# Four-layer network on one core: small VectorE steps of the two Mamba layers issued between a slot's product and its scan

## The chip, the cores and the metric

The kernel runs on one core of a Trainium2 chip (trn2). A core has five engines that run side by side, each in the order in which its own instructions were written, and each held up only by semaphores: TensorE (PE in the profile), VectorE (DVE), ScalarE (ACT), GpSimd (POOL) and SyncE (SP), which issues the transfers here. The metric is the device time of one execution in microseconds; lower is better. Three timed executions before the change took 11755.33, 11777.04 and 11796.26 us, the median is 11777.04 us.

## The reference, cut to what matters

Four images of 256 channels and 64x64 points go through four layers. Layers 0 and 1 are recurrences with windowed attention, which the change does not touch. Layer 2 is a Mamba layer with 512 inner channels, layer 3 runs one Mamba of 128 inner channels over four groups of 64 channels, with a small MLP and a convolution behind it. The core of both is this scan over the 4096 points, for 16 states n of every channel:

```
delta = softplus(dt @ dt_proj_w + dt_proj_b)
step:  h = exp(delta*A) * h + (delta*u) * B        # per state
       y = sum over states of h * C
y = (y + u*D) * silu(z)                            # the gate
```

In front of layer 2 and layer 3 stands a normalization over the channels, which subtracts the mean ("centring") and divides by the deviation.

## The kernel before, in words

An image goes through the layers alone; the four images follow one another. In both Mamba layers the points are cut into 4 chunks of 1024 (NC), and the inner channels of a chunk into 4 blocks of 128 partitions, so that a layer has 16 blocks. A block has 16 **slots**, one for each state: layer 2 and layer 3 of an image are 256 slots each, written out one after the other in `scan_blocks` (L907). A slot i is this work on [128, 1024] tiles:

- spread: TensorE copies row B of the state to all partitions, into a PSUM tile `pb` (L949); there are two such tiles, so spread(i+2) waits for scan(i).
- product: VectorE multiplies `pb` by `du` (delta times u) in place (L1019).
- decay: ScalarE computes `da` = exp(delta*A) three slots ahead (L961).
- scan: VectorE runs the recurrence over the 1024 points (L1025), reading `da` and `pb`.
- GpSimd multiplies the result `h` by C into `hc` (L1031); there are three `h` and three `hc` tiles.
- turn: TensorE adds `hc` into the PSUM tile `y` by eight transposes (L977), one slot later.

Three states of a block (0, 5, 10 in layer 2 and 0, 4, 8 in layer 3) are **apart**: their B row comes by a transfer, GpSimd does the product (L935), and the decay goes to PSUM as `dap`. Such a slot has no product on VectorE.

All other work is cut into small steps that are hung on slots by hand. `put(d, places, steps)` files a step under a slot number of a block; the loop runs the steps of a slot (`blk["bg"]`) after it has issued the slot's scan, so on VectorE such a step stands between the scan of its slot and the product of the next. A place n + 0.5 comes a little later in the slot. The steps that the change touches:

- `delta_steps` (L1139) makes delta for a later block in two halves of 512 columns: proj (a matmul into a PSUM tile `dt_ps`, then Abs, Exp and Ln on ScalarE, L1150 to L1152), add (one VectorE instruction, L1156, that reads `dt_ps`), and at last `times_u` (GpSimd, `du`, L1160).
- `end` (in `scan_blocks`) finishes the block before: at slot ends[0] ScalarE copies `y`; at slots ends[1] and ends[2] TensorE transposes a half back and adds u*D into a PSUM tile `fin_ps` (L998, L1002); one slot after each, VectorE multiplies it into the gate `zs` (L991). ends is (1, 2, 4) in layer 2 and (1, 2, 2) in layer 3.
- `norm_steps`: mean (matmul), center (VectorE, L1087, and a Square on ScalarE, L1093), deviation, scale, affine.
- `in_u` makes u of the next pair of blocks or chunk by matmuls (L1314 in layer 2, L1700 in layer 3), which a Silu, the x projection and delta of that block follow.

`dt_ps`, `fin_ps`, `u_ps`, `ln_pm`, `z_ps` and others share the PSUM tag "mm", which has two buffers. A matmul that needs one waits, and with it all that TensorE has behind it, until the last reader of the buffer's old content is done. In layer 3 `in_u` takes both at once:

```python
            def two(name):
                return [psum.tile([P, NT], F32, tag="mm", name=name) for g in range(2)]
```

Of the kernel before, what the change touches and what calls it, by code (L numbers as in the profile page):

```python
# [12 lines left out]
ALU = mybir.AluOpType  # L13
# [13 lines left out]
DS = 16  # L27
# [17 lines left out]
class Net:  # L45
# [858 lines left out]

    def scan_blocks(self, blocks, loop, psum, psb, psy, apart, ends, first, last={}):  # L907
        nc = self.nc
        slots = [(blk, n) for blk in blocks for n in range(DS)]
        halves = [slice(s, s + NT) for s in range(0, NC, NT)]  # L910
# [71 lines left out]

        def end(blk, n):
            if n == ends[0]:
                for ss in halves:
                    nc.scalar.activation(blk["du"][:, ss], blk["y"][:, ss], AF.Copy)
            for j, (ss, first) in enumerate(zip(halves, ends[1:])):
                if n == first + 1:  # L990
                    nc.vector.tensor_tensor(  # L991
                        blk["zs"][:, ss], blk["out", j], blk["zs"][:, ss], ALU.mult
                    )
                if n == first:
                    blk["out", j] = ps = psum.tile([P, NT], F32, tag="mm", name="fin_ps")
                    for i in range(NT // P):
                        t = slice(ss.start + i * P, ss.start + i * P + P)
                        nc.tensor.matmul(  # L998
                            ps[:, i * P : (i + 1) * P], blk["du"][:, t], self.ident,
                            is_transpose=True, start=(i == 0), stop=False,  # L1000
                        )
                    nc.tensor.matmul(ps, blk["diag_d"], blk["u"][:, ss], start=False, stop=True)  # L1002
# [14 lines left out]
        for i, (blk, n) in enumerate(slots):  # L1017
            if not is_apart(i):
                nc.vector.tensor_tensor(pb[i], blk["du"], pb[i], ALU.mult)  # L1019
            h[i] = loop.tile([P, NC], F32, tag="h", name="h", bufs=3)  # L1020
            for ss in pieces(i):
                state = 0.0 if blk["first"] else blk["state"](n)
                if ss.start:
                    state = h[i][:, ss.start - 1 : ss.start]
                nc.vector.tensor_tensor_scan(  # L1025
                    h[i][:, ss], da[i][:, ss], pb[i][:, ss], state, ALU.mult, ALU.add
                )
            product(i + 2)
            hc[i] = loop.tile([P, NC], F32, tag="hc", name="hc", bufs=3)
            for ss in pieces(i):  # L1030
                nc.gpsimd.tensor_tensor(hc[i][:, ss], h[i][:, ss], cb[i][:, ss], ALU.mult)  # L1031
            decay(i + 3)
            keep(i - 1)
            load_c(i + 3)
            load_b(i + 4)
            if i >= DS and n != ends[0]:
                end(slots[i - DS][0], n)
            for step in blk["bg"].get(n, ()):
                step()
            if i >= DS and n == ends[0]:  # L1040
                end(slots[i - DS][0], n)
            spread(i + 2)
            for step in blk["bg"].get(n + 0.5, ()):
                step()
            turn(i - 1)
            decay(i + 2, True)
            for d in (pb, da, cb):
                del d[i]
        turn(n_slot - 1)
        for n in range(ends[2] + 2):  # L1050
            end(blocks[-1], n)
            for f in last.get(n, ()):
                f()
# [168 lines left out]
    def mamba_layer(self, x, bridge, pe_dram, w_in, w_cw, w_x, w_dt, w_out, v_dram):  # L1222
        tc, nc = self.tc, self.nc
        ND = 4
        with ExitStack() as ctx:
# [232 lines left out]
            for k in range(n_chunk):  # L1458
# [3 lines left out]
                def put(d, where, steps):  # L1462
                    for i, f in zip(where, steps):
                        bg[d].setdefault(i, []).append(f)

                if k == 0:
                    put(0, (2, 3, 4, 5), folds)
                if k:
                    for i, where in enumerate(((3, 4, 5), (6, 7, 8), (9, 10, 11), (12, 13, 14))):
                        put(0, where, out_proj(k - 1, i // 2, i % 2))  # L1470
                put(0, (9, 10, 11, 12, 12), delta(k, 1))
                put(0, (14, 15), (in_z(k, 0, 0), in_z(k, 0, 1)))
                put(1, (1.5,), (silu((k, 0, "zs")),))
                put(1, (6, 7, 8, 9, 10), delta(k, 2))
                put(1, (11, 12), (in_z(k, 1, 0), in_z(k, 1, 1)))
                put(1, (14,), (silu((k, 1, "zs")),))
                at = (6, 7, 8, 9, 10) if more else (5, 6, 7, 8, 9)
                put(2, at, delta(k, 3))
                at = (10, 11) if more else (8, 9)
                put(2, at, (in_z(k, 2, 0), in_z(k, 2, 1)))  # L1480
                z3 = in_z(k, 3, 0), in_z(k, 3, 1)
# [4 lines left out]
                if more:  # L1486

                    if k == 0:
                        put(0, (0,), (lambda: begin(1),))
                        put(0, (0, 0, 1, 3, 4, 5, 6, 7), self.later(lambda: norm(1, 0), 8))  # L1490
                    h1 = self.later(lambda k=k: norm(k + 1, 1), 8)
                    if k:
                        put(0, (2, 4, 5, 7, 8, 13, 14, 15), h1)
                    else:
                        put(0, (7, 8, 9, 12, 13, 14, 15), h1[:7])
                        put(1, (1,), h1[7:])
                    if k + 2 < n_chunk:
                        put(3, (3,), (lambda k=k: begin(k + 2),))
                        h0 = self.later(lambda k=k: norm(k + 2, 0), 8)
                        put(3, (4, 6, 7, 14, 15), h0[:5])  # L1500
                        chunks[k + 1]["late"] = ((0, 1, 2), h0[5:])
                    if k:
                        put(0, *chunks[k]["late"])
                    u = all_u(k + 1)
                    put(1, range(5, 16), u[:11])
                    put(2, range(14), u[11:25])
                    put(3, (1, 2, 3, 4, 5, 5, 6), u[25:])
                    xs = x_proj(k + 1)
                    put(2, (13,), (silu((k + 1, 0, "u"), (k + 1, 1, "u"), (k + 1, 2, "u"),
                                        (k, 2, "zs")),))  # L1510
                    put(3, (7,), (silu((k + 1, 3, "u"), (k, 3, "zs")),))
                    put(3, (7, 8, 8, 9), xs)
                    put(3, (10, 11, 11, 12, 12), delta(k + 1, 0))
                    put(3, (10, 11, 12, 13), xs[4:])
                else:
                    put(2, (13,), (silu((k, 2, "zs"), (k, 3, "zs")),))

                    sums, about, square, squares, early_squares = stats

                    def square_into(i):  # L1520
                        tag, bufs = ("pe", 1) if i % 2 else ("u", 5)
                        square(i, work.tile([P, NC], F32, tag=tag, name="cs_sq", bufs=bufs))

                    for i in range(6):
                        put(1 + (13 + i) // DS, ((13 + i) % DS,), (lambda i=i: sums(i),))
                        put(2 + (12 + i) // DS, ((12 + i) % DS,), (lambda i=i: square_into(i),))
                        put(2 + (13 + i) // DS, ((13 + i) % DS,), (lambda i=i: squares(i),))
                    put(2, (3,), (about,))
                    put(3, (3,), (early_squares,))
                    for i in range(4):  # L1530
                        at = (6 + 2 * i, 7 + 2 * i)
                        put(3, at, out_proj(k, i // 2, i % 2, ((0, 1, 2),)))
# [18 lines left out]
            def center(s):  # L1551
# [6 lines left out]

            self.scan_blocks(
                [blk for c in chunks for blk in c["blocks"]], loop, psum, psb, psy, (0, 5, 10),  # L1560
                (1, 2, 4), (xs0[4:6], (), xs0[6:]),
                {1: [lambda: mean3(0)], 2: [lambda: center(0)], 4: [lambda: mean3(1)],
                 5: [lambda: center(1)]},
            )
            late_square, late_sums, late_squares, finish = late_stats
            sq3 = work.tile([P, 2, NC + 3], F32, tag="xn", name="ln_sq")
# [50 lines left out]
    def grouped_mamba_layer(self, x, bridge, begun, ws_dram, outc_dram, v_dram, out_b, load):  # L1617
        tc, nc = self.tc, self.nc
        w_in, w_cw, w_x, w_dt, w_out, w_f1, w_f2 = ws_dram
        with ExitStack() as ctx:  # L1620
# [359 lines left out]
            for i, (k, c) in enumerate(pairs):  # L1980
                even, odd = chunks[k]["blocks"][2 * c : 2 * c + 2]

                def put(blk, where, steps):
                    for i, f in zip(where, steps):
                        blk["bg"].setdefault(i, []).append(f)


                for where, steps in late:
                    put(even, where, steps)
# [3 lines left out]
                if more:  # L1993
                    h0, h1 = (self.later(lambda k=k, s=s: norm(k + 1, s), 5) for s in range(2))
                    put(even, (0,), (lambda k=k: begin(k + 1),))
                    put(even, (0, 1, 4, 5, 6), h0)
                    put(even, (14, 15), h1)
                    put(odd, (1, 2, 3), h1[2:])
                put(even, (4, 5, 9, 11, 12, 13) if i else (6, 7, 9, 11, 12, 13), x_proj(k, 2 * c + 1))
                if i:  # L2000
# [8 lines left out]
                        late.append(((0, 0.5, 1, 1), m1[4:]))  # L2009
                    else:  # L2010
                        put(odd, (3, 4, 4.5, 5, 6), m1[3:])
                put(even, (7, 9, 8, 9, 10) if i else (9, 10, 10, 11, 11), delta(k, 2 * c + 1))
                also = [lambda k=k: out_silu(k - 1)] if c == 1 and k else []
                if i == 0:
                    put(even, (1, 2), [in_z(0, 0, s) for s in range(2)])
# [13 lines left out]
                if i + 1 < len(pairs):  # L2029
# [1 line left out]
                    put(odd, (4, 5, 6, 7), all_u(nk, ncol))  # L2031
                    put(odd, (7,), (silu(nk, ncol, "u"),))
                    put(odd, (8, 8, 8, 9, 10, 11), x_proj(nk, 2 * ncol))
                    put(odd, (9, 11, 10, 11, 12), delta(nk, 2 * ncol))
                    put(odd, (13, 14), [in_z(nk, ncol, s) for s in range(2)])
            self.scan_blocks(
                [blk for c in chunks for blk in c["blocks"]], loop, psum, psb, psy, (0, 4, 8),
                (1, 2, 2), (xs0[2:4], (), xs0[4:]),
            )

            k, pair = n_chunk - 1, chunks[-1]["blocks"][2:]
# [160 lines left out]
```

## Time and profile before

| what | value |
|---|---|
| timed executions, median of 3 | 11777.04 us |
| the profiled execution, its own time | 11788.99 us |
| its span, first to last instruction | 11787.2 us |
| mean granted TensorE clock | 0.936 |
| busy TensorE, VectorE | 10026.0 us (85%), 9803.2 us (83%) |
| busy GpSimd, ScalarE | 8773.9 us (74%), 7025.7 us (60%) |
| scans of layer 2, first image | 978 to 1922 us of the span |
| scans of layer 3, first image | 1973 to 2923 us of the span |

The times are from one execution under the profiler, whose instructions are listed with start, length, the idle time of the engine before it, and what ended that idle time. An engine that is busy for a large share of the span need not set the time: what counts is which wait ends last in a stage. The two Mamba layers take 944 and 950 us of each image, so some 64% of the span over four images; the rest is attention.

### The profile page before, as it was taken

The numbers are of one execution on the slowest core, as the hardware profiler recorded it, in microseconds if no ns is written. First come the engines' busy times: TensorE is split into PE (matmuls) and PEld (weight loads), VectorE is DVE, ScalarE is ACT, GpSimd is POOL, SyncE is SP. The second block draws the span as 40 slices with busy tenths as digits, with TensorE's granted clock in tenths as the row PEclk, the third lists the DMA queues.
The fourth block names the chain that finished last, engine by engine and source line by source line (L and its number), as shares of the span: only waits on it lengthen the run. The fifth ranks groups of instructions, "written<-read, shape, count | busy, mean of one in ns | idle before, by whom it ended". The sixth has DMA issues, their size and how long they took to land. (4 is left out here: it accounts for less than half of the span.)

```text
span 11787.2 us, 192389 instructions
## 1 busy us (share of the span) xinstructions
PE 10026.0 (85%) x71104; PEld 5739.6 (49%) x71104; DVE 9803.2 (83%) x8342; ACT 7025.7 (60%) x13152; POOL 8773.9 (74%) x6070
## 2 busy tenths in 40 slices
PE   8998887777899888777789988877778998887787
PEld 4564554444456455444445645544444564554443
DVE  6677998998667799899866779989986677998998
ACT  4565555776456555577645655557764565555776
POOL 4666887898466688789846668878984666887897
PEclk9999998999999899899999989989999998998999
DMA  3344554454334455455433445545543354554554
GB/s 97 106 137 139 174 174 148 168 181 161 90 105 136 136 172 177 148 171 180 163 88 108 140 136 176 172 148 170 179 161 91 104 142 139 172 174 149 169 175 154
DMA packets 682507, 1742.11 MB, mean 148 GB/s; under 512 B 88896, under 2 KB 194896, under 8 KB 681312
## 3 DMA queue, kind: packets, MB, share of 16 engines
q1 hardware_dynamic: 676448, 1721.41, 44.9%
q8 instruction: 563, 9.22, 0.3%
q10 hardware_dynamic: 5120, 8.39, 0.3%
q14 instruction: 376, 3.08, 0.1%
HBM read 1601.52 MB, written 94.39 MB: 144 GB/s over the span
## 5 line engine op out<-in xcount | busy, mean ns | idle before, releaser
L1031 POOL TENSOR_TENSOR hc<-h,cb 128x1024 f32<-128x1024 f32 x2056 | 4809.8, 2351 | 785.8 <-DVE h L1025 332.9
L1025 DVE TENSOR_TENSOR_SCAN h<-da,m_state,pb 128x1024 f32<-128x1024 f32 x1248 | 2920.4, 2340 | 163.6 <-DVE pb L1019 3.4
L977 PE MATMUL y<-ident,hc 128*128 128x128 f32 x16384 | 2358.0, 292 | 413.2 <-POOL hc L1031 342.3
L977 PEld LDWEIGHTS y<-ident,hc 128*128 128x128 f32 x16384 | 2050.6, 151 | 1144.6 <-POOL hc L1031 598.5
L1019 DVE TENSOR_TENSOR pb<-du,pb 128x1024 f32<-128x1024 f32 x1672 | 2025.2, 1211 | 104.1 <-PE pb L949 97.4
L961 ACT ACTIVATE da<-delta,m_v 128x1024 f32<-128x1024 f32 x1672 | 1899.2, 1141 | 132.4 <-DVE h L1025 109.0
L949 PE MATMUL pb<-m_parts,pick 128*128 128x512 bf16 x3312 | 1083.0, 411 | 804.0 <-DVE h L1025 753.7
L603 POOL TENSOR_SCALAR pr<-pr,sm,zero 128x256 f32<-128x256 f32 x2048 | 1107.3, 556 | 384.5 <-DVE sm L600 380.3
L588 ACT ACTIVATE pr<-sc,mn 128x256 f32<-128x256 f32 x2048 | 953.1, 477 | 515.9 <-DVE sm L600 397.6
L949 PEld LDWEIGHTS <-pick 128*128 128x128 bf16 x3312 | 263.5, 101 | 1742.9 <-DVE h L1025 971.6
L577 DVE TENSOR_REDUCE mn<-sc 128x4 f32<-128x1024 f32 x512 | 630.1, 1232 | 536.1 <-PE sc L565 536.0
L1025 DVE TENSOR_TENSOR_SCAN h<-da,pb 128x1024 f32<-128x1024 f32 x424 | 969.7, 2287 | 54.5 <-DVE pb L1019 0.5
L935 POOL TENSOR_TENSOR bb<-du,bb 128x1024 f32<-128x1024 f32 x376 | 888.8, 2364 | 111.4 <-DMA bb<-m_cd 102.4
L1025 DVE TENSOR_TENSOR_SCAN h<-dap,m_state,bb 128x1024 f32<-128x1024 f32 x288 | 672.3, 2335 | 68.2 <-ACT dap L961 48.3
L252 PE MATMUL conv_ps<-att_y,att_wb 128*128 128x512 f32 x1536 | 685.9, 596 | 0.0
L616 PE MATMUL pt_ps<-ident,pr 128*128 128x128 f32 x4096 | 638.6, 292 | 41.9 <-POOL pr L603 21.8
L961 ACT ACTIVATE dap<-delta,m_v 128x1024 f32<-128x1024 f32 x376 | 419.8, 1117 | 313.7 <-DVE h L1025 232.2
L565 PE MATMUL sc<-kv,q_swap 32*64 32x128 f32 x8192 | 592.5, 282 | 15.6 <-DMA kv<-kv_dram 5.4
L565 PE MATMUL sc<-kv,att_y 32*64 32x128 f32 x7168 | 574.5, 282 | 33.3 <-DMA kv<-kv_dram 24.3
L616 PEld LDWEIGHTS pt_ps<-ident,pr 128*128 128x128 f32 x4096 | 459.5, 146 | 169.8 <-POOL pr L603 111.6
L290 DVE SCALAR_TENSOR_TENSOR lp<-vimg,att_v,lp 128x512 f32<-128x512 f32 x672 | 507.7, 756 | 30.8 <-DVE lp L290 1.0
L565 PEld LDWEIGHTS sc<-kv,att_y 32*64 32x64 f32 x7168 | 425.9, 136 | 165.2 <-ACT pr L588 76.6
(303 smaller groups left out, 17832.5 us busy)
## 6 DMA issues: line engine op xcount, KB each, us to landing
cb<-m_cd SPq DMA_DIRECT2D x2048, 512.0 KB, 3.9
kv<-kv_dram SPq DMA_DIRECT2D x1984, 128.0 KB, 2.8
bb<-m_cd SPq DMA_DIRECT2D x376, 512.0 KB, 5.1
kv_dram<-kst SPq DMA_DIRECT2D x128, 256.0 KB, 3.4
kv_dram<-vn SPq DMA_DIRECT2D x128, 256.0 KB, 4.1
q_swap<-att_y SPq DMA_DIRECT2D x96, 256.0 KB, 4.3
m_pe<-in_pe_dram SPq DMA_DIRECT2D x32, 512.0 KB, 5.9
out_dram<-yo SPq DMA_DIRECT2D x64, 256.0 KB, 2.4
```

What stands on the lines that cost most here:

```text
L252: nc.tensor.matmul(ps, w[:, k, w0 + m * P : w0 + (m + 1) * P], src[:, k], start=(k == 0), stop=(k == 1),)
L565: nc.tensor.matmul(sc[h][b * 64 : b * 64 + 64, r, w, m, :], (own(sj, m) if r == b else swap[sj % 2][:, m])[rows, 2 * a + w], kv[i, w][rows ...
L588: nc.scalar.activation(t[:, g].rearrange("p j r t -> p r j t"), sc[h][:, :, g // 2, g % 2, :].rearrange("p r (j t) -> p r j t", j=2), AF.E ...
L603: nc.gpsimd.tensor_scalar(t[:, g], t[:, g], s[:, g : g + 1], self.zero, ALU.mult, ALU.add)
L616: nc.tensor.transpose(pt[h][j][:, g, :], t[:, g, j].rearrange("p r t -> p (r t)"), self.ident,)
L935: nc.gpsimd.tensor_tensor(pb[i], slots[i][0]["du"], pb[i], ALU.mult)
L949: nc.tensor.matmul(pb[i][:, ss], self.pick[:, n : n + 1].to_broadcast([P, P]), blk["parts"][:, ss], start=True, stop=True,)
L961: nc.scalar.activation(da[i], blk["delta"], AF.Exp, scale=blk["a"](n))
L977: nc.tensor.matmul(blk["y"][:, ss], t[:, ss], self.ident, is_transpose=True, start=(n == 0 and ss.start % NT == 0), stop=(n == DS - 1 and ...
L1019: nc.vector.tensor_tensor(pb[i], blk["du"], pb[i], ALU.mult)
L1025: nc.vector.tensor_tensor_scan(h[i][:, ss], da[i][:, ss], pb[i][:, ss], state, ALU.mult, ALU.add)
L1031: nc.gpsimd.tensor_tensor(hc[i][:, ss], h[i][:, ss], cb[i][:, ss], ALU.mult)
```

## The change

In `scan_blocks` a new list of steps, filed under `("between", n)`, is run after slot n's product has been issued and before its scan; the gate products get a function of their own, run in the same place, with slots of their own (`gates`).

```diff
+        def gate(blk, n):
+            for j, (ss, at) in enumerate(zip(halves, gates)):
+                if n == at:
+                    nc.vector.tensor_tensor(
+                        blk["zs"][:, ss], blk["out", j], blk["zs"][:, ss], ALU.mult
+                    )
+
         def end(blk, n):
...
-                if n == first + 1:
-                    nc.vector.tensor_tensor(
-                        blk["zs"][:, ss], blk["out", j], blk["zs"][:, ss], ALU.mult
-                    )
...
             if not is_apart(i):
                 nc.vector.tensor_tensor(pb[i], blk["du"], pb[i], ALU.mult)
+            for step in blk["bg"].get(("between", n), ()):
+                step()
+            if i >= DS:
+                gate(slots[i - DS][0], n)
...
-        for n in range(ends[2] + 2):
+        for n in range(max(gates) + 1):
+            gate(blocks[-1], n)
             end(blocks[-1], n)
```

The two additions of delta, the gate products and some centrings are filed there. `soft` puts the five steps proj, add, proj, add, times_u, the two adds between:

```diff
+                def soft(d, places, steps):
+                    p0, a0, p1, a1, du = places
+                    put(d, (p0, ("between", a0), p1, ("between", a1), du), steps)
# layer 2
-                put(0, (9, 10, 11, 12, 12), delta(k, 1))
+                soft(0, (9, 11, 11, 13, 13), delta(k, 1))
-                put(1, (6, 7, 8, 9, 10), delta(k, 2))
+                soft(1, (6, 8, 8, 11, 11), delta(k, 2))
-                at = (6, 7, 8, 9, 10) if more else (5, 6, 7, 8, 9)
-                put(2, at, delta(k, 3))
+                at = (6, 8, 8, 10, 10) if more else (5, 7, 7, 9, 9)
+                soft(2, at, delta(k, 3))
-                        put(0, (2, 4, 5, 7, 8, 13, 14, 15), h1)
+                        put(0, (2, 4, 5, 7, ("between", 9), 13, 14, 15), h1)
-                        put(0, (7, 8, 9, 12, 13, 14, 15), h1[:7])
+                        put(0, (7, 8, 9, 12, ("between", 14), 14, 15), h1[:7])
-                    put(3, (10, 11, 11, 12, 12), delta(k + 1, 0))
+                    soft(3, (10, 12, 11, 13, 13), delta(k + 1, 0))
-                (1, 2, 4), (xs0[4:6], (), xs0[6:]),
+                (1, 2, 4), (4, 6), (xs0[4:6], (), xs0[6:]),
-                 5: [lambda: center(1)]},
+                 6: [lambda: center(1)]},
# layer 3
-                    put(even, (0, 1, 4, 5, 6), h0)
+                    put(even, (0, ("between", 2), 4, 5, 6), h0)
-                put(even, (7, 9, 8, 9, 10) if i else (9, 10, 10, 11, 11), delta(k, 2 * c + 1))
+                soft(even, (7, 9, 8, 10, 10) if i else (9, 11, 10, 12, 12), delta(k, 2 * c + 1))
-                    put(odd, (9, 11, 10, 11, 12), delta(nk, 2 * ncol))
+                    soft(odd, (9, 11, 10, 12, 12), delta(nk, 2 * ncol))
-                (1, 2, 2), (xs0[2:4], (), xs0[4:]),
+                (1, 2, 3), (4, 5), (xs0[2:4], (), xs0[4:]),
```

No instruction is added or removed and no tile changes its size; what changes is the order on VectorE, the slots of `times_u` in layer 2, and in layer 3 the slot of the second `fin_ps` and of its gate.

## The prediction

> **What bounds the kernel now.** I began with the page: busy shares, then the groups. The change works in the two Mamba layers alone, so what counts is what holds VectorE (DVE) between their scans.
>
> ```profile
> PE 10026.0 (85%) x71104; PEld 5739.6 (49%) x71104; DVE 9803.2 (83%) x8342; ACT 7025.7 (60%) x13152; POOL 8773.9 (74%) x6070
> L1025 DVE TENSOR_TENSOR_SCAN h<-da,m_state,pb 128x1024 f32<-128x1024 f32 x1248 | 2920.4, 2340 | 163.6 <-DVE pb L1019 3.4
> L1019 DVE TENSOR_TENSOR pb<-du,pb 128x1024 f32<-128x1024 f32 x1672 | 2025.2, 1211 | 104.1 <-PE pb L949 97.4
> ```
>
> The second line shows 163.6 us of idle time before 1248 scans, 131 ns each, of which only 3.4 us has a releaser: a gap in front of every scan that follows its product. The third shows that products wait for TensorE's spread, but only 97.4 us in all.
>
> The groups of VectorE with shapes kept apart show the steps that move. They stand idle for other engines before them:
>
> ```profile
> L1156 DVE SCALAR_TENSOR_TENSOR delta<-dt_ps,delta 128x512 f32<-128x512 f32 x256 | 171.6, 675 | 102.8 <-ACT delta L1152 102.8
> L991 DVE TENSOR_TENSOR m_zs<-fin_ps,m_zs 128x512 f32<-128x512 f32 x256 | 169.4, 674 | 56.1 <-PE fin_ps L1002 55.9
> ```
>
> The timeline of VectorE (start, length, both in us) shows the gap at close range:
>
> ```profile
> 1062.24 0.67 DVE L991 TENSOR_TENSOR m_zs<-fin_ps,m_zs 128x512 f32<-128x512 f32 x1
> 1062.83 1.22 DVE L1019 TENSOR_TENSOR pb<-du,pb 128x1024 f32<-128x1024 f32 x1
> 1064.18 2.29 DVE L1025 TENSOR_TENSOR_SCAN h<-da,pb 128x1024 f32<-128x1024 f32 x1
> 1066.38 2.26 DVE L1025 TENSOR_TENSOR_SCAN h<-dap,bb 128x1024 f32<-128x1024 f32 x1
> ```
>
> The gate ends at 1062.91, and the product starts 0.08 before that. The product ends at 1064.05, and the scan that reads it starts 0.13 later. The next scan starts 0.09 before the last one's end. So a pair of neighbours costs 0.21 to 0.22 us more when the second reads the first; I use 0.217 (133 ns after the end against 84 ns before it, the usual values along the timeline).
>
> Last, busy time by stretch, for one chunk (four blocks) of layer 2, cut where another engine takes over. Columns: stretch, its us, then busy us of PE, PEld, DVE, ACT, POOL, the clock, DMA.
>
> ```profile
> 4254.60:4351.80 97.20, 93.22 (x397) 52.35 (x398) 92.08 (x56) 52.85 (x83) 80.14 (x35) 0.98 0.51 173
> 4351.80:4379.20 27.40, 26.62 (x111) 15.54 (x112) 23.31 (x15) 13.18 (x24) 18.92 (x9) 0.94 0.50 181
> 4379.20:4425.70 46.50, 35.04 (x153) 20.72 (x152) 41.85 (x26) 28.88 (x45) 45.64 (x21) 0.89 0.51 167
> 4425.70:4490.60 64.90, 57.12 (x262) 33.32 (x260) 62.60 (x39) 39.34 (x62) 60.33 (x27) 0.97 0.51 179
> ```
>
> TensorE is full in the first two (in_u, 93.22 of 97.20 and 26.62 of 27.40), GpSimd in the third (45.64 of 46.50). VectorE sets the pace in the fourth alone: 65 of 236 us. That is the point of this case: VectorE's savings count only where nobody else is full.
>
> **The change, part by part.** *The swap.* Moved steps that get a product in front of them: in layer 2, per image, 27 adds, 30 gates and 3 centrings; in layer 3, 30 adds, 15 gates (the other 15 come before slot 4, which is apart and has no product) and 3 centrings. That is 108, over four images 432. Each puts an instruction between a product and its scan: 432 x 0.217 = 94 us of gaps, if all counted. Here a rule of the Trainium skill speaks against the change: VectorE: DVE Perf Modes, section "The DRAIN you can't avoid", says a flush follows every VectorE operation, that the next cannot start before it ends, and that this cannot be skipped; by it the order is worth 0. This trace starts an independent successor 84 ns before the end. No row has another operation between a product and its scan, but attention has the like: reduces (L365) that read a scan's result with one operation between show 0.0 us of idle time before 128 of them. I take 0.217, and keep 0 as the lower end.
>
> *The waits.* Along the timeline of the second image, waits of moved steps (beyond an overlapped start) sum to 4.3 us in layer 2 and 20.5 in layer 3: 24.8, so 99 us over four images. The rest of the 159 us in the two rows lies at the layers' beginnings and ends, where nothing is swapped. A product of 1.12 (1.21 less the overlap) fits into each; most are below that.
>
> *What counts in layer 2*, per chunk. Last stretch: six swapped steps (five in the chunk's first block, one gate in the next), 1.30, and a wait of 0.44 for ACT. Third: nothing. Second: TensorE, then one gate, 0.22. First: TensorE is full, but once it stands 0.68 at in_u for the second gate, whose buffer it is given; in the new order that gate comes later than in_u's turn, in_u finds the other buffer, which ScalarE has emptied, and the 0.68 goes. Sum 2.6. The last chunk has no in_u (VectorE busy 216.33 of 223.10 us by the same view): 14 swaps are 3.0, one wait 0.5. The first I put at 1.5. Layer: 1.5 + 2x2.6 + 3.5 = 10.2.
>
> *Layer 3* has a price. In odd blocks in_u starts at slot 4 and takes both "mm" buffers; one held the second fin_ps. Its gate stood before scan 4; now it comes after product 5, and in_u with all of TensorE's queue behind it (spread, turn) waits for it.
>
> ```profile
> 5232.24 1.26 DVE L991 TENSOR_TENSOR m_zs<-fin_ps,m_zs 128x512 f32<-128x512 f32 x2
> 5233.42 2.34 DVE L1025 TENSOR_TENSOR_SCAN h<-dap,m_state,bb 128x1024 f32<-128x1024 f32 x1
> 5235.68 1.21 DVE L1019 TENSOR_TENSOR pb<-du,pb 128x1024 f32<-128x1024 f32 x1
> ...
> 5235.38 1.99 PE L1700 MATMUL u_ps<-m_xn,m_wi 64*128 64x512 f32 x8
> ```
>
> New order: first gate 5232.24 to 5232.82, scan 4 to 5235.08, product 5 to 5236.2, second gate until 5236.9. in_u's second matmul, at 5235.6 before, comes at 5236.9: 1.3 late. TensorE then runs without a pause to the end of in_u, and ScalarE's Silu, x projection and delta follow without one, up to the second add of this block, which waited 1.2. So that add is ready 1.3 later; product 12, now in front of it, hides 1.34. Net 0 in such a block. In the odd blocks before a new chunk (5340 us on) in_u came at 5358.6, its second matmul at 5358.8, and by the same steps the gate would now end at 5359.85: 1.05 late, against 1.35 to 1.4 hidden, so 0.35 gained; the gates' waits there (0.65 and 0.61) lie ahead of the same chain and bring nothing. In even blocks in_u is absent: where GpSimd is full (52.91 of 53.00 us from 5296.7 to 5349.7) only the steps before slot 5 count, 0.8 (a gate moved behind scan 4, 0.58, and a centring); in the others two adds and a gate, 0.65, and a gate's wait of 0.55. A chunk: 1.2 + 0 + 0.8 + 0.35 = 2.35; the layer, with less in the first and last chunk, 8.
>
> *What else moves.* No moved step issues a DMA, so SP's queue keeps its order. On POOL `du` goes one slot later in layer 2 (12 to 13 at the latest); behind it stands the apart product issued in slot 14, which POOL reached after `du` before too: 0. On ACT a centring's Square waits a product longer, 1.1, and behind it stands the `da` that is read three slots (some 10 us) later: 0. In layer 2 a buffer released at "between n" is asked for in slot n at the earliest; TensorE there first does spread and turn, 1.5 us, against 1.7 for product and step, and its next spread waits for the scan anyway: 0.
>
> Sum: (10.2 + 8) x 4 = 73 us. The profiled execution took 11788.99 us (11787.2 of span), 12 above the median; from its time 11716, against the median 11777 this is 11704.
>
> **The rivals.** *All of it counts* (0.2): 94 + 99 = 193 us, 11584. For it: VectorE is busy 54.48 of 57.20 us in the block of layer 3 from 5161.9 us on, and its waits for others are short. Against: the full TensorE and GpSimd above.
> *Nothing counts* (0.17): the rule of the flush holds, or each saved gap ends in the next wait for spread, `dap` or `bb`: 11777. For it: the stretches above; against: the fourth one and each image's last chunk.
> *Slower* (0.1): the blocked in_u. If TensorE reaches in_u at slot 4 as soon as spread (two matmuls of 0.4) and turn (1.04) allow, 1.84 us after scan 3 ends, it waits for the second gate until 4.6 (gate 0.58, scan 2.26, product 1.12, gate 0.67), so 2.8; less the 1.35 hidden that is 1.4 lost in 28 odd blocks, 40 us, and if layer 2's gates hold TensorE likewise its 41 us are not earned: 11817. It decides once in_u's delay passes what product 12 hides, 1.35. Against it: in the block shown turn waited for GpSimd until 5234.36, so the delay is 1.3.
>
> **How the numbers follow.** The forecast has 0.53, with 11670 to 11740 as its own range. Eight in ten lie between 11620, between it and the first rival, and 11775, near no change. A measurement of this kernel tells about 0.3% (35 us) from no change; faster by more needs under 11742: nearly all of the forecast and the first rival, 0.72; within 0.3%: 0.18; slower 0.10.
>
> **What would show it.** Right: the idle time before L1025 with pb falls by some 90 us, that before L1156 and L991 falls below 60; layer 2 is about 10 us shorter per image, layer 3 about 8; in_u (L1700) newly waits for the gate (L991), about 1.3 us, 28 times. Wrong: scans behind a moved step keep a gap of 0.13; or waits for spread, `dap` and `bb` take up all that is saved, also in a last chunk; or layer 3 is longer than before, with the second add waiting more.

## The result, and the profile after

The change makes the kernel a little slower: median 11795.86 us (11779.55 to 11819.77, 19 runs) against 11773.12 us of the kernel before on the same chip (11755.01 to 11796.26, 19 runs). The ratio is 1.0020, 95% interval 1.0013 to 1.0028, so 23 us more where 73 fewer were forecast. That is inside what was called no change (35 us), but at 19 runs its sign is clear. The profiled execution has a span of 11777.8 us against 11787.2: one execution scatters by more than the effect, so below I compare the two Mamba layers' loops (first scan's start to last scan's end) and take times from many runs.

Page of the kernel after, busy time and two groups (columns as before; the product is now L1022, the scan L1032):

```profile
PE 9953.2 (85%) x70636; PEld 5707.2 (48%) x71104; DVE 9769.2 (83%) x8342; ACT 7029.8 (60%) x13152; POOL 8773.2 (74%) x6070
L1032 DVE TENSOR_TENSOR_SCAN h<-da,m_state,pb 128x1024 f32<-128x1024 f32 x1248 | 2917.3, 2338 | 122.1 <-DVE pb L1022 1.0
L1022 DVE TENSOR_TENSOR pb<-du,pb 128x1024 f32<-128x1024 f32 x1672 | 2023.6, 1210 | 236.7 <-PE pb L949 191.3
```

The groups of VectorE with shapes apart, additions (L1164) and gates (L988):

```profile
L1164 DVE SCALAR_TENSOR_TENSOR delta<-dt_ps,delta 128x512 f32<-128x512 f32 x256 | 174.3, 682 | 57.6 <-ACT delta L1160 57.3
L988 DVE TENSOR_TENSOR m_zs<-fin_ps,m_zs 128x512 f32<-128x512 f32 x256 | 174.0, 680 | 36.8 <-PE fin_ps L1005 36.5
```

The idle time that the change was to remove is smaller: scans 163.6 to 122.1, additions 102.8 to 57.6, gates 56.1 to 36.8. But the products' own idle time rose from 104.1 to 236.7 us, most of it for TensorE's spread (97.4 to 191.3). What was saved in front of the scans came back in front of the products.

The swap itself, in the timeline of VectorE after:

```profile
5475.47 1.21 DVE L1022 TENSOR_TENSOR pb<-du,pb 128x1024 f32<-128x1024 f32 x1
5476.58 0.68 DVE L1164 SCALAR_TENSOR_TENSOR delta<-dt_ps,delta 128x512 f32<-128x512 f32 x1
5477.18 2.34 DVE L1032 TENSOR_TENSOR_SCAN h<-da,m_state,pb 128x1024 f32<-128x1024 f32 x1
```

The addition starts 0.10 before the product ends, the scan 0.08 before the addition ends. Over all 432 swapped pairs in the trace the usual values are 91 and 84 ns of overlap.

By layer, mean of the four images' loops in us (one profiled execution each; the runs below are described in the next section):

| kernel | layer 2 | layer 3 | median of runs, ratio to before |
|---|---|---|---|
| before | 938.0 | 946.6 | 1 |
| after | 933.6 | 954.7 | 1.0020 |
| after, layer 3's gates as before (e3) | 934.2 | 940.6 | 0.9977 |
| e3, B's row first on SP's queue (e7; e11) | 927.2; 926.0 | 936.7; 936.9 | 0.9926; 0.9935 |
| after, B's row first (e10) | 926.6 | 958.4 | 0.9997 |
| before, B's row first (e9) | 934.5 | 942.7 | 0.9987 |
| before, layer 3's second gate moved (e12) | 936.0 | 959.6 | 1.0056 |

So layer 2 gains 4.4 us, not 10.2, and layer 3 loses 8.1 instead of gaining 8. In layer 3 the even blocks together went from 469.1 to 466.0 us, the odd ones from 477.5 to 488.7. Block by block, on the mean of the four images, the growth of the odd ones lies in blocks 5, 9 and 13 (2.5, 1.9 and 4.6 us), which hold in_u, and in block 15 (2.5 us), the layer's last, which holds none.

### The profile page after: what moved, and what is told of

The parts are those of the page before. It is cut to its first block, busy times and chain, and to the rows that moved or that the text cites. A ratio compares the mean times of both kernels' runs of the same rounds, so it can differ in the third digit from the quotient of the medians.

```text
span 11777.8 us, 192029 instructions
## 1 busy us (share of the span) xinstructions
PE 9953.2 (85%) x70636; PEld 5707.2 (48%) x71104; DVE 9769.2 (83%) x8342; ACT 7029.8 (60%) x13152; POOL 8773.2 (74%) x6070
## 5 line engine op out<-in xcount | busy, mean ns | idle before, releaser
L1032 DVE TENSOR_TENSOR_SCAN h<-da,m_state,pb 128x1024 f32<-128x1024 f32 x1248 | 2917.3, 2338 | 122.1 <-DVE pb L1022 1.0
L977 PE MATMUL y<-ident,hc 128*128 128x128 f32 x16384 | 2333.0, 290 | 533.7 <-POOL hc L1038 426.3
L1022 DVE TENSOR_TENSOR pb<-du,pb 128x1024 f32<-128x1024 f32 x1672 | 2023.6, 1210 | 236.7 <-PE pb L949 191.3
L949 PE MATMUL pb<-m_parts,pick 128*128 128x512 bf16 x2844 | 959.1, 407 | 736.6 <-DVE h L1032 697.2
L1032 DVE TENSOR_TENSOR_SCAN h<-da,pb 128x1024 f32<-128x1024 f32 x424 | 968.7, 2285 | 43.0 <-DVE pb L1022 1.4
L935 POOL TENSOR_TENSOR bb<-du,bb 128x1024 f32<-128x1024 f32 x376 | 888.1, 2362 | 137.5 <-DMA bb<-m_cd 130.2
L1032 DVE TENSOR_TENSOR_SCAN h<-dap,m_state,bb 128x1024 f32<-128x1024 f32 x288 | 672.9, 2337 | 97.8 <-ACT dap L961 47.9
```

The costliest lines, as they stand in the source:

```text
L935: nc.gpsimd.tensor_tensor(pb[i], slots[i][0]["du"], pb[i], ALU.mult)
L949: nc.tensor.matmul(pb[i][:, ss], self.pick[:, n : n + 1].to_broadcast([P, P]), blk["parts"][:, ss], start=True, stop=True,)
L977: nc.tensor.matmul(blk["y"][:, ss], t[:, ss], self.ident, is_transpose=True, start=(n == 0 and ss.start % NT == 0), stop=(n == DS - 1 and ...
L1032: nc.vector.tensor_tensor_scan(h[i][:, ss], da[i][:, ss], pb[i][:, ss], state, ALU.mult, ALU.add)
```

## The experiments

**Where the loss is (e1, e2).** The change in one layer alone; the other layer has the places of the kernel before (each edit cut to one place; "old gates" stands for gates issued after scan 3).

```diff
# e1: layer 3 as before           # e2: layer 2 as before
-  (1, 2, 3), (4, 5)              -  soft(1, (6, 8, 8, 11, 11), delta(k, 2))
+  (1, 2, 2), old gates           +  put(1, (6, 7, 8, 9, 10), delta(k, 2))
```

> The change in layer 2 alone; layer 3 in its old order. Both theories of the loss (A: the second gate holds in_u up in layer 3's odd blocks; B: TensorE at half speed after its idle stretches in layer 3's odd blocks) put the loss in layer 3, so both expect before minus what layer 2's loops got shorter by in the two traces, 17.6 us: about 11755 us. If the loss were a drift of the whole program (the other rival, C: the order on VectorE is worth nothing and the rest is chance), 11773 as before.

> The change in layer 3 alone. A and B: before plus what layer 3's loops got longer by, 32 us: about 11805 us. C: as before, 11773. The sum of the two halves' differences should come to the +23 us of the whole change; if it doesn't, one layer's order shifts the other's.

e1: 11766.85 us, ratio 0.9994 (0.9985 to 1.0002): 7 us less where 18 were expected, and not told from no change. e2: 11829.12 us, 1.0052 (1.0038 to 1.0066): 61 us of loss where 32 were expected. So the loss is layer 3's. But the two differences sum to 54 us and the whole change loses 23: the halves don't simply add. Part of it is seen in the traces: among blocks 5, 9 and 13 of the four images, which take 60.7 to 62.5 us or over 65 (below), seven are of the long kind in e2 and four in the whole change, some 13 us. Why, and the rest, stays open.

**The gate that holds in_u up (e3, e12).** Waits of TensorE in the trace after (who waited for whom: total us, times, longest):

```profile
PE u_ps L1712 <- DVE m_zs L988: 19.7, 25, 1.4
```

This row is new; the kernel before has none for layer 3's in_u. The waits are 1.0 to 1.44 us in most blocks 5, 9 and 13 and about 0.3 in the odd blocks before a new chunk. The timeline of TensorE shows one case, in the odd block that the prediction took as its example, one chunk on:

```profile
5445.46 1.12 PE L1712 MATMUL u_ps<-m_xn,m_wi 64*128 64x512 f32 x2
5448.02 1.95 PE L1712 MATMUL u_ps<-m_xn,m_wi 64*128 64x512 f32 x6 [1.44 <-DVE m_zs L988]
```

e3 issues both final products in slot 2 again and both gates ahead of scan 4. As slot 4 is apart, that is their old order; the rest of the change stays. e12 is the reverse: the kernel before, with this move alone (both edits cut).

```diff
# e3, in the change                 # e12, in the kernel before
-  (1, 2, 3), (4, 5)                -  (1, 2, 2), old gates
+  (1, 2, 2), (4, 4)                +  (1, 2, 3), (4, 5)
```

> The change, but in layer 3 both final products are issued in slot 2 again and both gates stand between product 4 and scan 4, so that in_u finds both of its buffers released before scan 4 ends. A: the waits of products 6 and 9 (0.5 and 0.13 us, in blk 13 up to 2.4 and 0.4) and the growth at 10 and 11 go, about 1.5 us in each of 28 odd blocks, so 11796 - 42 = about 11754 us. B: the wait for the gate was only one idle stretch of several, product 2 still waits 0.7 to 2.7 us: 11780 to 11796.

> The kernel before with one part of the change alone: in layer 3 the second final product goes from slot 2 to slot 3 and the gates stand before scan 4 and between product 5 and scan 5; all additions, centrings and layer 2 as before. A: the whole loss comes with this, and no saved gap of the additions stands against it: in_u 1.3 us late in 28 odd blocks, the second addition as late (no product in front of it hides it), TensorE slow after the wait in some; 11776 + 52 or more, so 11825 to 11850 us. Rival G (the loss needs the additions' new order too, the gate alone is hidden): 11776 to 11790.

e3: 11744.0 us, 0.9977 (0.9971 to 0.9984), about 50 us below the change and faster than before. e12: 11837.5 us, 1.0056 (1.0042 to 1.0069), 66 us above before by the ratio. Both fit A, that the moved gate is the cause; the rival G falls, since the move costs no less without the additions than with them. In e3's timeline in_u's first eight matmuls run in one piece:

```profile
5440.08 1.99 PE L1712 MATMUL u_ps<-m_xn,m_wi 64*128 64x512 f32 x8
```

Why does a wait of 1.44 us cost so much? VectorE of the kernel after, the rest of the same block (idle time and its releaser in brackets):

```profile
5450.55 1.23 DVE L1022 TENSOR_TENSOR pb<-du,pb 128x1024 f32<-128x1024 f32 x1 [0.42 <-PE pb L949]
...
5465.75 1.23 DVE L1022 TENSOR_TENSOR pb<-du,pb 128x1024 f32<-128x1024 f32 x1 [1.89 <-PE pb L949]
...
5470.97 1.23 DVE L1022 TENSOR_TENSOR pb<-du,pb 128x1024 f32<-128x1024 f32 x1 [1.52 <-PE pb L949]
5472.61 0.69 DVE L1164 SCALAR_TENSOR_TENSOR delta<-dt_ps,delta 128x512 f32<-128x512 f32 x1 [0.41 <-ACT delta L1160]
```

These are products 6, 10 and 11, and then the first addition. In the same block of the kernel before, products 6 and 10 don't wait; product 11 does:

```profile
5496.88 1.23 DVE L1019 TENSOR_TENSOR pb<-du,pb 128x1024 f32<-128x1024 f32 x1 [1.40 <-PE pb L949]
```

So the wait at product 11 is not the change's. Over the 28 odd blocks with in_u, product 10 waits 2.73 us on the mean, against 0.84 before, 0.95 in e3 and 2.84 in e12; product 6 waits 0.74, against 0.03, 0.11 and 0.54; product 11 waits 0.45, against 0.60 before. TensorE ahead of product 10:

```profile
5463.29 1.98 PE L1765 MATMUL x_ps<-m_u,m_wx 128*128 128x512 f32 x4 [2.31 <-ACT m_u L1744]
5465.11 0.59 PE L949 MATMUL pb<-m_parts,pick 128*128 128x512 bf16 x2
```

Spread 10 stands behind the x projection, which waits for the Silu of in_u's result. So in_u's delay does not travel to the second addition alone: it reaches VectorE at products 6 and 10, ahead of product 12, which was to hide it.

In block 15 the late gate holds up something else: the first matmuls of the MLP (`f_ps`), behind which spread 5 is queued. TensorE and VectorE of the kernel after, second image:

```profile
5807.68 1.12 PE L1801 MATMUL f_ps<-m_sq,m_wf 64*128 64x512 f32 x2 [1.76 <-DVE m_zs L988]
5809.58 2.03 PE L1801 MATMUL f_ps<-m_sq,m_wf 64*128 64x512 f32 x2 [0.78 <-ACT hid L1808]
5811.55 1.04 PE L949 MATMUL pb<-m_parts,pick 128*128 128x512 bf16 x2
```

```profile
5812.62 1.23 DVE L1022 TENSOR_TENSOR pb<-du,pb 128x1024 f32<-128x1024 f32 x1 [2.74 <-PE pb L949]
```

Product 5 of this block waits 2.2 to 2.7 us in all four images, and 1.8 to 2.7 in e12; in the kernel before and in e3 it doesn't wait. That is some 10 us of the loss.

**TensorE at half clock (e4, e5, e6, e8).** In three odd blocks (5, 9 and 13) the time differs from image to image. Block 13 takes 65.8 us in three images and 61.2 in the fourth. The timeline of TensorE shows why; here is the start of block 9, then in_u of block 13:

```profile
5427.66 1.01 PE L949 MATMUL pb<-m_parts,pick 128*128 128x512 bf16 x2 [2.19 <-DVE h L1032]
...
5430.86 1.97 PE L977 MATMUL y<-ident,hc 128*128 128x128 f32 x8
...
5689.86 3.43 PE L1712 MATMUL u_ps<-m_xn,m_wi 64*128 64x512 f32 x6 [1.44 <-DVE m_zs L988]
```

The eight transposes that elsewhere take 1.04 take 1.97, and in_u's six matmuls 3.43 instead of 1.95. The stretches of the kernel after (stretch, its us, then busy us of PE, PEld, DVE, ACT, POOL, the granted clock, DMA) name it: the clock is 0.51 for these us, and 1.00 right after.

```profile
5427.60:5434.30 6.70, 6.64 (x16) 2.99 (x16) 5.82 (x3) 4.76 (x6) 6.70 (x4) 0.51 0.32 118
5434.30:5441.00 6.70, 5.35 (x32) 2.90 (x33) 4.72 (x4) 3.40 (x9) 5.30 (x4) 1.00 0.75 274
5689.80:5696.00 6.20, 5.81 (x17) 2.97 (x18) 3.74 (x3) 0.00 (x0) 4.58 (x3) 0.53 0.60 231
```

To take this away I gave TensorE work where it idles: products of a zero matrix, added into `y`. e4 has seven at the end of even blocks and five (its text says four) ahead of in_u; e5, e6 and e8 have six at the end of even blocks, in e3's kernel, in the change and in the kernel before.

```diff
+            def fill(blk, count):
+                def step():
+                    for j in range(count):
+                        nc.tensor.matmul(
+                            blk["y"][:, first[j % 2]], self.none,
+                            self.pick[:, 0:1].to_broadcast([P, NT]), start=False, stop=False,
+                        )
...
# ahead of the other steps of slot 15 in even blocks, count 6
```

> The change, with products of a zero matrix added on TensorE where it idles in layer 3 and adding zero to y: seven at the end of each even block (ahead of slot 15's spread, where it idled 1.7 to 2.5 us) and four ahead of in_u in slot 4 of the odd ones. B: TensorE no longer falls to half speed there, product 2's wait of 0.7 to 2.7 us in odd blocks and the slow u_ps of blk 13 go: about 1.5 us in each of 28 odd blocks, 11796 - 42 = about 11754 us. A: in_u still waits for the gate, and the added matmuls take time of their own: 11790 to 11810.

> The change as it is with the same six products of a zero matrix at the end of the even blocks, and nothing before in_u. B: product 2's wait goes, in_u still waits for the gate: blks 5, 9 and 13 of layer 3 fall from 61.5, 62.5 and 65.8 to about 60.5 us, so 8.5 us a layer, 11796 - 34 = 11762 us. A alone: 11796 less nothing.

> Both gates of layer 3 before scan 4 (as in the run of 11744 us), and six products of a zero matrix on TensorE at the end of each even block of layer 3, adding zero to y, in the 2.4 us in which it would idle ahead of slot 15's spread. A and B together (the gate's wait and the half-speed phase are two costs): product 2 of the odd blocks no longer waits 0.8 to 2.4 us; at about 1.6 in three of four such blocks, 20 us, so 11724 us. A alone: 11744, the wait at product 2 only moves on to product 10.

> The kernel before with the same six products of a zero matrix in layer 3. Here product 2 hardly waits (in 2 of 12 odd blocks, 2 us each) and products 10 and 11 do. B as a cost of the change's new timing: 11765 to 11775. B as a cost of both kernels: below 11755.

e6's timeline and its stretch at that place (its lines stand two further down in the code):

```profile
5426.62 1.47 PE L1995 MATMUL y<-pick,none 128*128 128x512 bf16 x6
5429.18 0.59 PE L951 MATMUL pb<-m_parts,pick 128*128 128x512 bf16 x2 [1.09 <-DVE h L1034]
```

```profile
5429.10:5435.80 6.70, 6.42 (x29) 3.09 (x30) 6.38 (x4) 5.11 (x8) 6.70 (x4) 1.00 0.36 116
```

The clock stays at 1.00, and blocks 5, 9 and 13 take 60.5 to 60.6 us in all four images, as expected, where they took 60.7 to 65.9. In time: e6 11777.89 us, ratio 0.9995 (0.9987 to 1.0004), 0.25% below the change, some 29 us of the 34 expected. e4: 11770.8, 0.9999 (0.9990 to 1.0007), a gain of 25 where 42 were expected; the five products ahead of in_u took 1.25 us of TensorE's time there. e5: 11748.72, 0.9970 (0.9957 to 0.9982), not told from e3's 0.9977: the 20 us expected did not come, and the wait at product 2 indeed moved on to product 10. e8: 11783.08, 1.0003 (0.9994 to 1.0012): nothing, as expected for a cost of the new timing. So the half clock at these places is no cost of its own: it costs with the gate late (e6), and nothing with the gate in its old place (e5, e8). With the gate late it is some 29 of the 50 us that putting the gate back is worth.

**Layer 2's missing gain (e7, e9, e10, e11).** Layer 2's chunks, from first scan to first scan (the last one to the end of its last scan), went from 242.2, 236.7, 234.7 and 224.4 us to 239.4, 236.5, 236.4 and 221.3: the first and last gain, the two middle ones don't. The first and the last of four stretches of the kernel after, cut at the same slots as those of the prediction:

```profile
4227.60:4325.10 97.50, 92.07 (x390) 52.61 (x396) 91.63 (x56) 52.72 (x82) 81.67 (x35) 0.98 0.51 173
...
4399.20:4463.20 64.00, 55.53 (x259) 32.52 (x262) 62.45 (x39) 39.20 (x63) 57.91 (x26) 1.00 0.52 176
```

The last stretch is shorter by 0.9 us, less than the 1.74 summed for it, and the first, which begins with in_u, is 0.3 longer. GpSimd and SP's queue at the seam of the two stretches, block 9 (from two views of the timeline):

```profile
4460.99 2.36 POOL L935 TENSOR_TENSOR bb<-du,bb 128x1024 f32<-128x1024 f32 x1 [1.51 <-DMA bb<-m_cd]
```

```profile
4441.20 13.99 SPq L925 DMA_DIRECT2D cb<-m_cd  x4
4455.24 0.42 SPq L931 DMA_DIRECT2D bb<-m_cd  x1
```

GpSimd, the full engine, stands 1.51 us for a B row. That row is issued at 4455.24, behind C's rows, and C's rows wait for a buffer that GpSimd's own `hc` must release. The waits of SP's queue put 5903.4 us down to that:

```profile
SPq L925 <- POOL hc L1038: 5903.4, 1883, 10.9
```

TensorE then, waiting for `hc`, comes late to in_u, and with a slow clock; product 7 on VectorE, whose spread stands behind it, waits:

```profile
4465.71 1.97 PE L977 MATMUL y<-ident,hc 128*128 128x128 f32 x8 [1.95 <-POOL hc L1038]
4467.47 3.62 PE L1322 MATMUL u_ps<-m_xn,m_wxi 128*128 128x512 f32 x4
```

```profile
4471.89 1.23 DVE L1022 TENSOR_TENSOR pb<-du,pb 128x1024 f32<-128x1024 f32 x1 [2.19 <-PE pb L949]
```

In VectorE's terms the row comes later than before: in blocks 5 and 9 of all four images it is issued 5.7 us after scan 1 of the block starts, against 3.9. GpSimd waited for it there in the kernel before too (0.3 to 2.0 us), but products 7 and 8 did not wait; after, they wait 0.2 to 2.2 and 0.56 us. The edit swaps two issues in the loop:

```diff
-            load_c(i + 3)
-            load_b(i + 4)
+            load_b(i + 4)
+            load_c(i + 3)
```

e7 has it in e3's kernel, e9 in the kernel before, e10 in the change. e11 is e7 with layer 3's gates written after scan 3.

> Both gates of layer 3 before scan 4, and on SP's queue B's row for a slot on POOL loaded ahead of C's row of the same turn instead of behind it. Theory D (layer 2's missing gain: SP's queue is held by C's rows, which wait for POOL, so B's row lands 1.5 us late in blks 5 and 9, POOL and with it the transposition before in_u come late, products 7 and 8 wait 1.4 to 2.9 us): these waits go, 3 us in each of 8 blocks, 11744 - 20 = about 11724 us. Theory E (POOL is full there anyway, the row's time is no cost): 11744.

> The kernel before, with B's row loaded ahead of C's row on SP's queue. D (the row comes late because the change lets VectorE run ahead of POOL): hardly a gain here, 11770 to 11785 us. F (the row is late in both kernels, and the order on SP's queue is worth the same 47 us in both, the trace of before showing POOL waiting for the row some 24 us in each layer 3 and 4 in each layer 2): 11785 - 47 = about 11738 us, and then the change explains none of it.

> The change as it is, with B's row loaded ahead of C's. If the queue's cost and the gate's cost (A) add up: 52 us above the 11697 us of the run with both mended, 11750 us, and layer 3's products 6 and 9 still wait 0.5 and 0.13 us in odd blocks. If the late row was also what let the gate hold in_u up: 11700 to 11720.

> B's row ahead of C's, layer 3's gates where the kernel before has them (both after scan 3, so read and followed by a product), everything else as in the change. What differs from the run of 11697 us is the place of layer 3's two gates alone: between scan 3 and product 4, or between product 4 and scan 4. If a swapped pair is worth 0.217 us (one pair for the two gates, 15 blocks, 4 images): 13 us more, 11710. If the gates' place is worth nothing: 11697.

e7: 11697.36 us, ratio 0.9926 (0.9912 to 0.9940): 60 us below e3 by the ratios (47 by the medians, which come from two chips), more than the 20 expected. GpSimd's product of the apart slots on the pages of the kernel after and of e7, idle time last:

```profile
L935 POOL TENSOR_TENSOR bb<-du,bb 128x1024 f32<-128x1024 f32 x376 | 888.1, 2362 | 137.5 <-DMA bb<-m_cd 130.2
```

```profile
L935 POOL TENSOR_TENSOR bb<-du,bb 128x1024 f32<-128x1024 f32 x376 | 887.7, 2361 | 1.6 <-DMA bb<-m_cd 0.4
```

The same place of block 9 in e7, TensorE:

```profile
4458.29 1.09 PE L977 MATMUL y<-ident,hc 128*128 128x128 f32 x8 [0.40 <-POOL hc L1038]
4459.22 1.88 PE L1322 MATMUL u_ps<-m_xn,m_wxi 128*128 128x512 f32 x4
```

Products 7 and 8 no longer wait, and block 9 of layer 2 takes 55.5 to 55.6 us in all four images, against 56.8 to 57.1 before and 58.6 to 60.1 after. e9: 11761.03 us, 0.9987 (0.9979 to 0.9995). In the kernel before the same edit is worth 15 us, more than D's "hardly a gain" and a third of F's 47, though GpSimd waited 102.4 us for rows there too (130.2 after). e10: 11775.22 us, 0.9997 (0.9989 to 1.0005), above the 11750 expected: the edit is worth 27 us in the change as it is, and with the row mended the late gate costs 0.6 to 0.7% (e10 against e11 and e7), 73 to 84 us, not 52. Layer 2's middle chunks answer the question of this section: the edit shortens them by 0.1 and 0.2 us in the kernel before, and by 3.1 and 3.2 in the change. There the row was late in both kernels, and cost VectorE time only with the change, as D had it. In the first chunk and in layer 3 the edit gains in the kernel before as well, as F had it. The e11 expectation rests on a slip: slot 4 is apart and has no product, so e11's order on VectorE, ScalarE and GpSimd is that of e7. Its 11706.42 us, 0.9935 (0.9920 to 0.9950), is a second measurement of the same version.

e7 (with e11) beats both kernels: 0.65 to 0.74% below before, some 76 to 87 us.

## Why the prediction was wrong, step by step

- **The swap's size: right.** 0.217 us a pair was taken; 91 and 84 ns of overlap in 432 pairs, against a gap of 133 ns, confirm it, and the value 0 that the prediction drew from the flush rule falls; the same section of the page limits that rule itself, in a sentence the prediction passed over (an operation that is not held starts earlier). One line of "what would show it" was wrong by its own numbers: only the 133 ns are idle time, 57 us, the other 84 ns are overlap. The row fell by 41.5 us, the like row of first blocks (without m_state) by 11.5.
- **The waits of moved steps: right in kind.** Both rows fell below 60, to 57.6 and 36.8 us, some 64 of the 99 us counted.
- **Layer 2, 10.2 us: the potential was right, the earning wrong.** The 0.68 us that in_u stood for the second gate did go: that row is absent after. The fourth stretch's 1.74 came as 0.9, and 2.6 a middle chunk came as 0.2 and -1.7. The step that failed is the sentence that no moved step issues a DMA, "so SP's queue keeps its order", which put the queue at nothing. The order is kept, but B's row, behind C's rows that wait for GpSimd, is issued 5.7 us after scan 1 instead of 3.9, and products 7 and 8 of blocks 5 and 9 wait for what hangs on it. With B's row first, layer 2 is 10.8 us shorter than before (927.2 against 938.0; 3.5 of it the same edit brings in the kernel before).
- **Layer 3, odd blocks "net 0": the step that cost the sign.** in_u's wait for the gate was forecast as 1.3 us in 28 blocks; it came 25 times, at most 1.44 us, 0.79 on the mean and 1.16 in the block of the example. Wrong was where it ends: product 12 was to hide it ahead of the second addition, but spread 10 is queued on TensorE behind x_ps and carries it to product 10, which waits 1.9 us longer than before, and product 6 waits 0.7 longer. On top come the half clock and the last block's MLP, in no step of the prediction. Odd blocks before a new chunk (3, 7, 11) stayed within 0.5 us of before, near the forecast. Odd blocks together: +11.2 us a layer, and -6.5 against before once the gate is back (e3).
- **Layer 3, even blocks: half right.** Forecast were 1.2 and 0.8 in the two of a chunk. The first kind came: blocks 4, 8 and 12 gained 1.6, 0.8 and 1.3 us on the mean of the images. The second did not: blocks 2, 6, 10 and 14, where GpSimd was seen to be full, got 0.2 longer. In sum 3.1 us a layer, not some 8. The moved gate brings the gain, as the step had it: e12 has it too (465.2 us), e3 doesn't (469.6).
- **The rival on the slower side** named the mechanism (blocked in_u) and 11817 us; its condition, a delay past the 1.35 that product 12 hides, was the wrong test. It was given 0.10.

In sum: forecast -73, measured +23. Putting the gate back is worth 50 us, and B's row first some 60 on top by the ratios. What is then left of the swaps, e7 and e11 against e9, is 55 to 64 us by the medians, 61 to 72 by the ratios. That is near the 73 forecast for the whole change, but partly by luck: layer 3's gates, which made most of the forecast for its even blocks, stand in their old order there.

Open: why the two halves of the change don't add. In_u moved one slot later, behind the late gate, was not tried, nor a place for layer 3's second gate that is swapped and still early.

## What to carry to other kernels

When an instruction is moved later by one place, follow what it releases through every in-order queue behind the waiter, to the first instruction of the bounding engine that stands behind it; a cover farther down does not count. Do it for the last block too, where other work asks for the same buffers. A queue whose own order is unchanged can still fall behind if it waits for an engine that the change lets fall behind: put the transfer that a full engine needs ahead of one that waits for that engine.

## What the hardware showed

TensorE's granted clock was 0.51 over 6.7 us behind an idle stretch of 2.19 us, and 0.53 over 6.2 us behind one of 1.44 us. The Trainium skill, TensorE: Matmul & The Clock Gate, section "HAM oscillation — how this bites in real kernels", warns of idle gaps above about 3.4 us; here shorter ones sufficed at times. They don't always: in the kernel before, 2.43 us of idle time at the same place of block 9 was followed by a clock of 1.00:

```profile
5458.20:5463.00 4.80, 4.70 (x20) 2.01 (x20) 4.25 (x3) 4.14 (x6) 4.80 (x4) 1.00 0.28 103
```

The same page's section "What's actually happening" says the activity window runs free of the program, which would make it a matter of phase. The clock records of these traces agree: the clock is 1.0 or 0.5, and all its changes in an execution lie on one grid of 3.41 us, shifted by 0.16 us against the span's start in the kernel after and by 2.90 us in the kernel before. Of the grid's windows at full clock, those in which TensorE was busy for less than 0.40 were all followed by half clock (154 after, 171 before), those above 0.80 never (in e6 5 of 146 and 2 of 2169 went against this); in between it went either way, and what decides there is open. In the kernel after, the 2.19 us lay in one window, busy for 0.45; in the kernel before, the 2.43 us were split over two, busy for 0.52 and 0.74. Added zero products of 1.47 us, which left an idle stretch of 1.09, kept the clock up, and brought time only where TensorE was already the late one.
